# Idle TensorE products where the planned schedule leaves it resting, with newly searched turns

## The chip, the core and the metric

The kernel runs on one core of a Trainium2 chip. The metric is the device time of one execution in microseconds (us); the kernel before took 2129.86 us in the median of five runs (2125.64 to 2135.88). Engines are named as in the profile: PE is TensorE (PEld its weight loads), ACT ScalarE, DVE VectorE, POOL GpSimd, SP the engine that issues most DMAs. All data is float32 but for two bf16 masks.

## The reference, cut to what matters

Sixteen images of 512 tokens by 256 features pass through four layers, each added to its input:

```python
x = x + attention(layernorm(x))   # RMS norm, 16 heads of 16, causal softmax, output projection
x = x + routed(layernorm(x))      # base product + shared low-rank + 2 of 6 low-rank experts
x = x + scan(layernorm(x))        # conv of 4, silu, softplus step, 16-state recurrence, gate, projection
x = x + routed(layernorm(x))
```

The recurrence is `h = decay * h + inp` over the 512 tokens for each of 256 x 16 (feature, state) pairs, summed over states with `ct`.

## The kernel before, in words

All images are recorded as small operations, each with an engine, an estimated cost, the buffers that it reads and writes, and a function that issues its instructions. `Plan.order` then plays these operations through a model of the engines: whenever an engine is free it takes the ready operation with the lowest turn whose buffers are free. A turn is the image's entry in `STARTS` plus the operation's entry in `TURNS`, one list for all sixteen images; both lists, and `OVER` and `CHANGE`, come from a search made elsewhere. The functions are called in the order in which the model started them, and every engine's queue holds its instructions in that order. A few set-up operations (constants, weights, masks: `first`, `for_attention`, `for_routing`, `for_scan`) are issued ahead of the first operation of their stage; the model gives them no time.

PSUM has eight banks: four belong to the one buffer "sc", which holds the scores of four heads, and four to the four buffers "one", which serve everything else: projections, transposes, the sums of the scan and the decays. The tile layer gives each new "one" tile a bank whose old tile has had its last use issued, and adds the semaphore wait for that use. The planner counts free "one" buffers by its own clock.

What an image does, with the lines that matter here:

- Normalisation: VectorE statistics (L490, L491) for attention, ScalarE squares with a running sum (L507) for the other layers, a few GpSimd operations, then the scaled copy on ScalarE (L518: xhA, xhR). PE transposes it (L529), ScalarE copies it out (L532).
- Attention: projections (L480, called from several places), then for each of four groups of four heads the scores in two forms. `four` issues four 32-row products (L603) and four mask products (L605) into "sc". In the first form (sc from kT and qT) VectorE takes the row maxima (L677, negm); in the second (sc from qm and kT) ScalarE takes the exponential (L623, pt). As there is one "sc", PE can start the next scores only when VectorE or ScalarE has read the last. Between them PE does other work: weights by values (L630), transposes (L641, L685, L702), projections of other images.
- Routed layer: low-rank products (L480, low), some twenty tiny VectorE operations (L751 to L785), a transpose (L794), products with base and up (L480), VectorE adds (L558 or L554).
- Scan: conv and gate, then the step (dt) and step times input (sg, GpSimd L857) are stored to DRAM (drows), and fetched again, spread over 16 states (dd, L889 fetches of 512 KB). For each of 16 pieces GpSimd multiplies (L896), ScalarE makes two decays into "one" banks (L901), VectorE scans twice (L904), GpSimd multiplies (L907), and PE sums over states (L914, four products of two pieces), after which the pieces' dd buffers (five) are free for the next fetches.

Up to four images are under way at once, in different layers. The first image starts alone, and the last two end alone.

Of the kernel before, what the change touches and what calls it, by code (L numbers as in the profile page):

```python
# [10 lines left out]
F32 = mybir.dt.float32  # L11
# [6 lines left out]
P = 128  # L18
NEG = -1.0e30


OVER, CHANGE = 1.8, 98.0
STARTS = (
    0, 250, 450, 689, 961, 1201, 1411, 1675, 1928, 2203, 2451, 2680, 2957, 3175, 3503, 3764,
)
TURNS = (
    1486, 1502, 1591, 1805, 1649, 1220, 1616, 1672, 1410, 1613, 1491, 1898, 1583, 1875, 1343, 1506, 1183,
    1541, 1298, 1279, 1375, 1335, 1139, 1347, 1441, 1286, 1157, 1394, 1206, 1565, 1353, 1537, 1379, 1591,
    1379, 1594, 1372, 1651, 1522, 1660, 1365, 1611, 1517, 1583, 1349, 1403, 1398, 1378, 1448, 1325, 1481,
    1454, 1333, 1736, 1548, 1735, 1337, 1438, 1477, 1301, 1523, 1408, 1545, 1447, 1179, 1692, 1501, 1819,  # L30
    1508, 1490, 1586, 1319, 1422, 1542, 1547, 1376, 1572, 1477, 1589, 1287, 1623, 1386, 1700, 1560, 1706,
    1428, 1741, 1547, 1867, 1565, 1751, 1595, 1618, 1381, 1444, 1396, 1117, 1466, 1413, 1505, 1210, 1206,
    1711, 1675, 1808, 1463, 1423, 1594, 1561, 1499, 1404, 1606, 1475, 1396, 1802, 1678, 1811, 1675, 1644,
    1851, 1522, 1400, 793, 1319, 860, 713, 1017, 1032, 632, 724, 538, 935, 830, 973, 723, 927, 594, 796,
    525, 755, 598, 976, 661, 615, 1198, 512, 319, 388, 362, 129, 494, 312, 358, 602, 524, 567, 502, 544,
    859, 531, 746, 681, 561, 1231, 1218, 1194, 538, 729, 790, 1427, 1103, 1044, 704, 1086, 1098, 1018, 922,
    1615, 1327, 2057, 999, 2302, 1044, 1268, 1651, 1845, 1952, 2206, 1645, 1707, 2356, 1737, 1676, 1481,
    1017, 1153, 1270, 1220, 1217, 1026, 1092, 1419, 1470, 1474, 1403, 1419, 1405, 1245, 1447, 1465, 1366,
    1442, 1300, 1587, 1537, 1510, 1358, 1604, 1638, 1487, 1692, 1620, 1552, 1539, 1145, 1320, 1419, 1331,
    1542, 1656, 1715, 1772, 1728, 1673, 1650, 1876, 1677, 1609, 1610, 1726, 1779, 1751, 1778, 1654, 1464,  # L40
    1718, 1712, 1847, 1789, 1885, 1661, 1808, 1754, 1719, 2223, 1692, 1819, 1816, 1845, 1871, 1647, 1629,
    1805, 1577, 1758, 1803, 1893, 1944, 1483, 1819, 2065, 1596, 1989, 1718, 1866, 1889, 1718, 1723, 1901,
    1720, 1771, 1593, 1791, 1958, 1949, 1640, 1816, 1941, 1928, 1937, 1864, 1964, 2028, 1588, 1877, 2140,
    2072, 2032, 1799, 2052, 2224, 2260, 2139, 2353, 2400, 2267, 2365, 2277, 2293, 2410, 1995, 2248, 2295,
    2162, 2168, 1967, 2274, 2187, 2133, 1808, 2013, 2045, 2260, 2318, 2449, 2528, 2408, 2021, 2064, 2097,
    2119, 2019, 1819, 2261, 2249, 1936, 1316, 1929, 1436, 1226, 1471, 1322, 1474, 1422, 922, 1141, 1098,
    836, 1016, 1544, 1086, 1351, 1132, 1480, 1505, 2021, 1951, 1888, 2774, 1677, 1136, 1141, 936, 0, 876,
    507, 1665,
)


# [18 lines left out]
class Plan:  # L70
# [5 lines left out]

    def __init__(self, places):  # L80
        self.places, self.ops, self.seq, self.stage = dict(places), [], 0, 0
# [47 lines left out]
    def order(self):  # L129

        first = {}
        for o in self.ops:
            o.turn = STARTS[o.seq] + (TURNS or [0] * len(self.ops))[o.num - first.setdefault(o.seq, o.num)]
        free, busy, table, link, port, mode = dict(self.places), {}, None, 0.0, False, None
        kept = {}
        ready = {}
        for o in self.ops:
            ready.setdefault(o.eng, [])
            busy.setdefault(o.eng, False)
            if not o.left:  # L140
                bisect.insort(ready[o.eng], (o.turn, o.num, o))
        events, out = [], []
        now, tick = 0.0, 0
        while True:
            for eng, heap in ready.items():
                if busy[eng] or not heap:
                    continue
                until, what = kept.get(eng, (None, None))

                picked, turns = None, heap  # L150
                if eng == "ACT":
                    turns = sorted(heap, key=lambda i: (i[0] + CHANGE * (i[2].table not in (None, table)), i[1]))
                for item in turns:
                    if until is not None and not self.wanted(item[2], what):
                        cost = item[2].cost + 1.3 * (item[2].table not in (None, table))
                        if now + cost > until + OVER:
                            continue
                    need = {}
                    for b in item[2].bufs:
                        if not b.taken:  # L160
                            need[b.res] = need.get(b.res, 0) + 1
                    if not (item[2].port and port) and all(free[k] >= v for k, v in need.items()):
                        picked = item[2]
                        heap.remove(item)
                        break
                if picked is None:
                    continue
                o = picked
                for b in o.bufs:
                    if not b.taken:  # L170
                        b.taken = True
                        free[b.res] -= 1
                cost = o.cost
                if o.table is not None:
                    cost += 1.3 * (o.table != table)
                    table = o.table
                if eng == "PE":
                    cost -= 0.2 * (o.mode is not None and o.mode == mode)
                    mode = o.mode
                if until is not None and self.wanted(o, what):  # L180
                    del kept[eng]
                if isinstance(o.then, Op):
                    kept[o.then.eng] = (now + cost + o.lat, o.then)
                elif o.then is not None:
                    kept[o.then[0]] = (now + cost + o.lat, o.then[1])
                busy[eng] = True
                port = port or o.port
                out.append(o)
                end = now + cost
                done = end + o.lat  # L190
                if o.load:
                    link = max(link, end) + o.load
                    done = link + o.lat
                tick += 2
                heapq.heappush(events, (end, tick, "free", o))
                heapq.heappush(events, (done, tick + 1, "done", o))

            late = [eng for eng, (at, what) in kept.items() if at + 0.3 < now and not busy[eng]]
            for eng in late:
                del kept[eng]  # L200
            if late:
                continue
            if not events:
                if not kept:
                    break
                kept.clear()
                continue
            now = events[0][0]
            while events and events[0][0] <= now:
                _, _, kind, o = heapq.heappop(events)  # L210
                if kind == "free":
                    busy[o.eng] = False
                    if o.port:
                        port = False
                    continue
                for b in o.bufs:
                    b.users -= 1
                    if not b.users:
                        free[b.res] += 1
                for x in o.after:  # L220
                    x.left -= 1
                    if not x.left:
                        bisect.insort(ready[x.eng], (x.turn, x.num, x))
        assert len(out) == len(self.ops), "operations wait for each other's places"
        self.span = now
        return out


@with_exitstack
def tile_block(ctx: ExitStack, tc: tile.TileContext, a: dict, out: bass.AP):  # L230
# [4 lines left out]
    nc = tc.nc  # L235
# [16 lines left out]
    ps = ctx.enter_context(tc.tile_pool(name="ps", bufs=1, space=PSUM))  # L252
# [5 lines left out]
    def tile_of(name, shape, dtype=F32):  # L258
        return const.tile(shape, dtype, name=name)
# [7 lines left out]
    ident, identb = tile_of("ident", [P, P]), tile_of("identb", [P, P], BF)  # L267
# [166 lines left out]
    banks = {"one": (4, [P, 512]), "sc": (1, [P, G, 512])}  # L434
# [3 lines left out]
    plan = Plan(places)  # L438
# [497 lines left out]
    with tc.manual_schedule():  # L936
        done = 0
        for o in plan.order():

            while done < o.stage:  # L940
                setups[done]()
                done += 1
            o.fn()


# [44 lines left out]
```

## Time and profile before

| what | value |
|---|---|
| median of five runs | 2129.86 us (2125.64 to 2135.88) |
| the profiled execution, its time | 2125.51 us |
| its span, first to last instruction | 2123.7 us |
| mean granted TensorE clock | 0.922 of full |
| PE busy | 1810.3 us (85%), 13253 matmul records |
| VectorE, ScalarE, GpSimd busy | 1400.6 (66%), 1292.8 (61%), 1411.0 us (66%) |
| PE's scores L603 waiting for pt L623 | 126.9 us, 105 times |
| PE's scores L603 waiting for negm L677 | 19.9 us, 17 times |
| PE's sums L914 waiting for dd L907 | 43.7 us, 14 times |
| stores of finished images issued (first, thirteenth, last) | 389.9, 1821.7, 2119.9 us |

Times in the profile count from the span's start. A float32 product that isn't a transpose leaves two matmul records, and a record's duration contains the end of its pipeline, so that records overlap. In the views by window, each row gives the busy time of five engines with the number of instructions, the mean granted clock (PEclk, 1.00 is full), the busy share of the DMA engines and GB/s. In a timeline each row gives start, duration, engine, line, operation, tiles, count, and in brackets how long the engine rested before and what ended it. Images are counted from 0.

### The profile page before, as it was taken

The numbers are of one execution on the slowest core, as the hardware profiler recorded it, in microseconds if no ns is written. First come the engines' busy times: TensorE is split into PE (matmuls) and PEld (weight loads), VectorE is DVE, ScalarE is ACT, GpSimd is POOL, SyncE is SP. The second block draws the span as 40 slices with busy tenths as digits, with TensorE's granted clock in tenths as the row PEclk, the third lists the DMA queues.
The fourth block names the chain that finished last, engine by engine and source line by source line (L and its number), as shares of the span: only waits on it lengthen the run. The fifth ranks groups of instructions, "written<-read, shape, count | busy, mean of one in ns | idle before, by whom it ended". The sixth has DMA issues, their size and how long they took to land. (4 is left out here: it accounts for less than half of the span.)

```text
span 2123.7 us, 35012 instructions
## 1 busy us (share of the span) xinstructions
PE 1810.3 (85%) x13253; PEld 983.1 (46%) x13253; DVE 1400.6 (66%) x2351; ACT 1292.8 (61%) x2077; POOL 1411.0 (66%) x846
## 2 busy tenths in 40 slices
PE   4679888999999998999998999999999998986534
PEld 2335354545454454545454454545455454544212
DVE  4224576858767686858767676858767676866462
ACT  2226567575767667676667667575667667664521
POOL 2001585858678585959678695848679585959593
PEclk8769899999999999999999999999999999998756
DMA  3000775939395685849395775939396785859591
GB/s 90 1 1 1 170 171 139 213 93 231 83 225 133 170 197 131 219 101 228 90 213 128 187 182 134 216 96 220 86 213 144 171 198 131 209 129 216 141 218 43
DMA packets 113066, 316.37 MB, mean 149 GB/s; under 512 B 17809, under 2 KB 36610, under 8 KB 112898
## 3 DMA queue, kind: packets, MB, share of 16 engines
q1 hardware_dynamic: 112194, 313.99, 61.4%
q8 instruction: 105, 1.72, 0.4%
q14 instruction: 63, 0.52, 0.1%
q10 hardware_dynamic: 704, 0.14, 0.0%
HBM read 287.87 MB, written 26.21 MB: 148 GB/s over the span
## 5 line engine op out<-in xcount | busy, mean ns | idle before, releaser
L904 DVE TENSOR_TENSOR_SCAN dd<-one,dd 128x512 f32<-128x512 f32 x512 | 611.3, 1213 | 138.0 <-POOL dd L896 50.0
L896 POOL TENSOR_TENSOR dd<-dd,bc 128x1024 f32<-128x1024 f32 x256 | 602.7, 2357 | 128.7 <-DMA dd<-drows 107.3
L907 POOL TENSOR_TENSOR dd<-dd,bc 128x1024 f32<-128x1024 f32 x256 | 602.8, 2357 | 52.5 <-DVE dd L904 48.1
L677 DVE TENSOR_REDUCE negm<-sc 128x4 f32<-128x512 f32 (+3 forms) x256 | 380.0, 1484 | 341.6 <-PE sc L605 340.7
L901 ACT ACTIVATE one<-dd,am 128x512 f32<-128x512 f32 x512 | 343.2, 689 | 180.4 <-DVE dd L904 88.1
L623 ACT ACTIVATE pt<-sc 128x2048 f32<-128x2048 f32 (+3 forms) x256 | 315.8, 1234 | 195.7 <-PE sc L605 195.1
L603 PE MATMUL sc<-qm,kT 32*128 32x512 f32 (+3 forms) x2048 | 227.4, 516 | 131.2 <-ACT pt L623 111.5
L603 PE MATMUL sc<-kT,qT 32*128 32x128 f32 (+3 forms) x2048 | 219.8, 500 | 33.3 <-DVE negm L677 16.8
L605 PEld LDWEIGHTS <-identb 128*128 128x128 bf16 x2048 | 121.6, 101 | 240.5 <-issue 228.2
L914 PE MATMUL one<-dd,ysel 128*32 128x512 f32 x1024 | 172.2, 675 | 43.8 <-POOL dd L907 43.7
L603 PEld LDWEIGHTS sc<-qm,kT 32*128 32x128 f32 x2048 | 86.2, 197 | 232.3 <-ACT pt L623 163.8
L503 POOL TENSOR_SCALAR mv<-sums 128x4 f32<-128x4 f32 x48 | 9.3, 194 | 253.4 <-DVE x L558 253.3
L630 PE MATMUL one<-pt,vv 128*32 128x512 f32 (+3 forms) x2048 | 170.1, 477 | 3.3 <-DVE dd L904 3.1
L507 ACT ACTIVATE xhR<-x,mv 128x256 f32<-128x256 f32 x192 | 95.1, 497 | 89.3 <-POOL mv L503 89.3
L603 PEld LDWEIGHTS sc<-kT,qT 32*128 32x128 f32 x2048 | 84.7, 194 | 125.8 <-DVE negm L677 36.4
L480 PE MATMUL one<-base,xtR 128*128 128x256 f32 x512 | 137.7, 392 | 0.0
L857 POOL TENSOR_TENSOR sg<-dt,xc 128x512 f32<-128x512 f32 x32 | 40.5, 1266 | 145.9 <-ACT dt L852 145.9
L630 PEld LDWEIGHTS one<-pt,vv 128*32 128x32 f32 x2048 | 63.7, 117 | 100.9 <-issue 79.8
L518 ACT ACTIVATE xhR<-x,nm,rs 128x256 f32<-128x256 f32 x192 | 100.8, 591 | 14.5 <-POOL nm L514 14.3
L558 DVE SCALAR_TENSOR_TENSOR x<-one,x 128x256 f32<-128x256 f32 x192 | 72.7, 416 | 55.4 <-PE one L480 55.3
L605 PE MATMUL sc<-mask_k,identb 128*128 128x128 bf16 x1024 | 109.0, 233 | 0.0
L605 PE MATMUL sc<-mask_q,identb 128*128 128x128 bf16 x1024 | 104.9, 227 | 0.0
(138 smaller groups left out, 2620.4 us busy)
## 6 DMA issues: line engine op xcount, KB each, us to landing
dd<-drows SPq DMA_DIRECT2D x512, 512.0 KB
x<-in_x_dram SPq DMA_DIRECT2D x16, 512.0 KB
drows<-dt SPq DMA_DIRECT2D x32, 256.0 KB
drows<-sg SPq DMA_DIRECT2D x32, 256.0 KB
bc<-brows SPq DMA_DIRECT2D x16, 512.0 KB
out_dram<-x SPq DMA_DIRECT2D x16, 512.0 KB
brows<-few SPq DMA_DIRECT2D x16, 64.0 KB
wo<-in_Wo_dram SPq DMA_DIRECT2D x2, 256.0 KB
```

The source lines that it names most:

```text
L480: nc.tensor.matmul(o[:, lo:hi], lhsT=lhsT, rhs=rhs, start=n == 0, stop=n == len(todo) - 1)
L518: op("ACT", act(256) + 0.18, lambda t=t: nc.scalar.activation(xh()[:, t, :], x()[:, t, :], AF.Identity, bias=nm()[:, t, 0:1], scale=rs()[: ...
L603: nc.tensor.matmul(sc()[:, g, 0:n], lhsT=lhsT(g), rhs=rhs(g), start=True, stop=False)
L605: nc.tensor.matmul(sc()[:, g, at : at + P], lhsT=identb, rhs=mask, start=False, stop=True)
L623: o.then = op("ACT", act(G * n), lambda pt=pt, sc=sc, n=n: nc.scalar.activation(pt(), sc()[:, :, 0:n], AF.Exp), r=[sc], w=[pt], table="exp")
L630: nc.tensor.matmul(av()[rows(g), kt * P : T], lhsT=vals()[:, kt, G * j + g, :], rhs=pts[kt]()[:, g, :], start=kt == 0, stop=kt == NT - 1,)
L677: o.then = op("DVE", dve(G * n), lambda t=t, n=n, sc=sc, nm=nm, s=s: nc.vector.tensor_reduce(nm()[:, t, :, 1 - s, 0:1], sc()[:, :, 0:n], A ...
L896: op("POOL", pool(1024), lambda dd=dd: nc.gpsimd.tensor_tensor(dd()[:, :, 1, :], dd()[:, :, 1, :], both(0), ALU.mult), port=True, r=[(bc, ...
L901: op("ACT", act(512) + 0.07, lambda i=i, k=k, dd=dd, dec=dec: nc.scalar.activation(dec(), dd()[:, i, 0, :], AF.Exp, scale=am[:, k + 4 * i ...
L904: op("DVE", 1.22, lambda i=i, dd=dd, dec=dec: nc.vector.tensor_tensor_scan(dd()[:, i, 1, :], dec(), dd()[:, i, 1, :], 0.0, ALU.mult, ALU.a ...
L907: op("POOL", pool(1024), lambda dd=dd: nc.gpsimd.tensor_tensor(dd()[:, :, 1, :], dd()[:, :, 1, :], both(1), ALU.mult), port=True, r=[(bc, ...
L914: nc.tensor.matmul(sums()[rows(g), :], lhsT=ysel[:, m, :], rhs=four[g]()[:, g % 2, 1, :], start=m == 0, stop=m == 3)
```

## The change

Two things change. First, `Plan.order` notes when PE works and how many "one" buffers are free by its own model, and a new method, `resting`, puts idle products into PE's planned rests: one wherever 0.45 us and a margin of 0.1 us are left before the next PE operation, a "one" buffer is free by the model for that long, and PE has worked for less than 72% of the last 3.4 us. When the operations are issued, each PE operation is preceded by its idle products: an identity times two copies of itself (256 columns, float32) into a fresh "one" tile that nothing reads. Second, `STARTS`, `TURNS`, `OVER` (1.8 to 1.9) and `CHANGE` (98 to 115) are new.

```diff
+    SPAN, BUSY, IDLE, EDGE = 3.4, 0.72, 0.45, 0.1
...
+                        if b.res == "one":
+                            room.append((now, free["one"]))
...
+                if eng == "PE":
+                    runs.append((now, end, o))
...
+        self.rests = self.resting(runs, room)
         return out
+
+    def resting(self, runs, room):
+
+        rests, last, at, k = {}, [], 0.0, 0
+        for begin, end, o in runs:
+            while at + self.IDLE + self.EDGE <= begin:
+                while k + 1 < len(room) and room[k + 1][0] <= at:
+                    k += 1
+                i, free = k + 1, room[k][1]
+                while i < len(room) and room[i][0] < at + self.IDLE + self.EDGE:
+                    free = min(free, room[i][1])
+                    i += 1
+                last = [x for x in last if x[1] > at - self.SPAN]
+                worked = sum(b - max(a, at - self.SPAN) for a, b in last)
+                if free > 0 and worked < self.BUSY * self.SPAN:
+                    rests[o.num] = rests.get(o.num, 0) + 1
+                    last.append((at, at + self.IDLE))
+                    at += self.IDLE
+                else:
+                    at += self.EDGE
+            last.append((begin, end))
+            at = max(at, end)
+        return rests
...
+            for _ in range(plan.rests.get(o.num, 0) if done else 0):
+                one = ps.tile([P, 512], F32, tag="one", name="one", bufs=banks["one"][0])
+                nc.tensor.matmul(one[:, 0 : 2 * P], lhsT=ident, rhs=ident.unsqueeze(1).to_broadcast([P, 2, P]), start=True, stop=True)
             o.fn()
```

In the built program 379 idle products stand in 115 runs between 8227 products of before: 18 between the set-up products and the first transposes, and one after those; 42 in the rest of the first image's lone attention; 32 while the pipeline fills; nine per image from image 3 to image 14 (four, one, two and two, always ahead of the same four operations); 15 in the last attention; and 163 in the drain, in runs of up to 21. In the middle each queue's order differs from before in a few exchanges alone: for some pieces of the scan the two halves or two neighbouring pieces change places on all five engines, and a value projection, a pair of transposes and some products move past a neighbour. The number of the other instructions of each kind is the same.

## The prediction

> **What bounds the kernel now.** I read the page's slices first: how busy TensorE (PE) is and which clock it was granted, each slice 53 us.
>
> ```profile
> PE   4679888999999998999998999999999998986534
> ...
> PEclk8769899999999999999999999999999999998756
> ```
>
> PE is at 90% from slice 6 to slice 36, while no other engine passes 80% for long. The clock is low in slices 2 to 4, lowest at the end, and just under full between. So I cut the span at the marks where the work changes (windows view: us, busy time and instructions of PE, PEld, DVE, ACT, POOL, then clock, DMA share, GB/s): opening, first attention alone, filling, twelve like periods between two stores of the result, and the drain.
>
> ```profile
> 0.00:40.10 40.10, 18.28 (x97) 11.06 (x97) 19.44 (x65) 13.08 (x21) 15.54 (x32) 1.00 0.47 119
> 40.10:165.00 124.90, 90.05 (x628) 42.83 (x628) 33.45 (x32) 31.51 (x35) 0.00 (x0) 0.71 0.00 1
> 165.00:389.87 224.87, 197.25 (x1495) 103.92 (x1493) 139.20 (x237) 138.81 (x219) 127.23 (x73) 0.92 0.53 127
> 389.87:1821.67 1431.80, 1315.00 (x9939) 720.09 (x9937) 1041.79 (x1729) 970.58 (x1560) 1055.13 (x624) 0.96 0.68 164
> ...
> 1941.00:2123.70 182.70, 88.53 (x320) 46.44 (x320) 83.80 (x150) 63.45 (x115) 122.93 (x67) 0.67 0.61 143
> ```
>
> What does a lost clock cost? The twelve periods answer it; two of them:
>
> ```profile
> 865.63:982.67 117.04, 106.61 (x831) 58.74 (x829) 86.84 (x145) 80.83 (x130) 87.25 (x53) 1.00 0.69 167
> 982.67:1103.37 120.70, 111.17 (x832) 61.08 (x829) 86.67 (x145) 81.08 (x130) 89.15 (x53) 0.94 0.68 162
> ```
>
> Same work, and only PE's busy time and the clock differ: the period at full clock takes 117.04 us, the mean is 1431.80/12 = 119.32. Where the clock falls, a finer cut shows why. In steps of 3.41 us, the grid on which the clock changes here:
>
> ```profile
> 1064.13:1067.54 3.41, 1.42 (x16) 0.55 (x14) 0.00 (x0) 3.41 (x7) 1.93 (x3) 1.00 1.04 229
> 1067.54:1070.95 3.41, 3.41 (x28) 2.85 (x28) 0.00 (x0) 2.60 (x5) 1.18 (x2) 0.50 1.04 231
> 1070.95:1074.37 3.42, 3.42 (x52) 1.55 (x48) 2.79 (x3) 3.39 (x6) 2.14 (x1) 1.00 1.05 232
> ```
>
> A step with PE busy 1.42 of 3.41 us is followed by one at half clock, a full one by full clock; the period's other poor step, 1077.78 to 1081.19, has 1.75. Over the whole span 47 full-clock steps are followed by half clock, and the busiest of them had 1.95 us; to come back, a half-clock step had to be busy 2.8 us or more. The rests come from the one "sc" place: PE waits for ScalarE to read the scores (in the waits view, sc L603 behind pt L623: 126.9 us in 105 waits).
>
> **The change, part by part.** *Where the products stand.* I set the place of each of the 379 products against the timeline of before. From 40 to 1941 us, 197 of them stand where PE rested: per period four before the scores of 128 columns (rest 1.99 us), one before those of 256 (1.52), two before those of 384 (1.11), two before the next head's first scores (0.87). An idle product is one like value's (L480, 128x256): eight records, four products, took 1.95 us, so (1.95 - 0.38)/7 = 0.22 us a record, two records, 0.45 us; at half clock 0.85 (a 128-column record at half clock: (1.91 - 0.42)/7 = 0.21 in the opening's transposes below; twice as wide and two of them). Four fill 1.8 of 1.99 us: they fit, with the 0.16 us by which a record outlasts its streaming. The two poor steps rise to 1.42 + 1.8 = 3.2 and 1.75 + 0.45 = 2.2 us busy, both over 1.95, so I expect the clock to hold.
>
> *Price of a half-clock microsecond.* The five periods at 0.94 (120.70 to 121.48) average 121.14 us, with 0.06 x 2 x 121.1 = 14.5 us at half clock: (121.14 - 117.04)/14.5 = 0.28 us each. The five at 0.97 average 118.29: 1.25/7.1 = 0.18.
>
> *Opening: +8.* 18 products stand ahead of the first transposes. But PE does not rest there:
>
> ```profile
> 18.80 2.08 PE L480 MATMUL one<-wo,sg 128*128 128x256 f32 x4 [0.64 <-DMA cw<-in_conv_w_dram]
> 20.67 1.91 PE L529 MATMUL one<-ident,xhA 128*128 128x128 f32 x8
> ```
>
> The transposes follow without a rest; ScalarE had their input at 10.7 us, for the set-up products held PE (the plan has no set-up in its time). 0.21 us a 128-column record shows half clock until about 23 us: 2.8 products in 2.4 us, 15.2 at 0.45: 9.2 us, less 0.9 as the transposes then run at full clock. All of image 0 waits for them. Ends: 7.2 (all at full clock, less 0.9) and 15.3 (all at 0.85).
>
> *First attention: -16.* Clock 0.71: 0.29 x 2 x 124.9 = 72 us at half clock. Its rests (36 us in the timeline) get 42 products. 72 x 0.28 = 20, and I count four fifths as recovered. Ends: -6 (0.18 and half of it) and -26 (half of the 52 us that PE is busy in them).
>
> *Filling: -8.* 0.08 x 2 x 224.9 = 36 us at half clock, x 0.23. Ends -3 and -10.
>
> *Twelve periods: -18.* All at 117.04: 12 x 2.28 = -27. Against it stands a new wait. A bank's new tile waits for the last reader of the old one; the second product before the 384-column scores gets the bank of a scan. In the full-clock period:
>
> ```profile
> 961.78 2.34 DVE L904 TENSOR_TENSOR_SCAN dd<-one,dd 128x512 f32<-128x512 f32 x2 [0.84 <-ACT one L901]
> ...
> 962.78 0.93 PE L603 MATMUL sc<-qm,kT 32*128 32x384 f32 x8 [1.11 <-ACT pt L623]
> ```
>
> That scan, first of the two in the new order, ends at 963.0; the product then ends at 963.45, and the scores come 0.67 us late. The product before the 256-column scores waits for a scan ending at 960.33: 960.78 instead of 960.63. Together 0.8 us a period, 12 x 0.8 = +9.6. Behind PE stand all later products, so it counts in full. Ends: 0 and 2.8 us a period (the pair's 2.34 and a product). The exchanges in the orders (which half of a scan pair goes first, on all five queues) leave counts and ScalarE's table loads (76) as they are; I take them at 0, within 1 us a period either way.
>
> *Drain: +9.* 163 products in 19 runs, 73 us in 107 us of rests; but they stand in order behind scans. At the last long run:
>
> ```profile
> 2079.82 1.92 PE L914 MATMUL one<-dd,ysel 128*32 128x512 f32 x4 [7.21 <-POOL dd L907]
> 2084.42 1.93 PE L914 MATMUL one<-dd,ysel 128*32 128x512 f32 x8 [2.68 <-POOL dd L907]
> 2086.99 1.63 PE L914 MATMUL one<-dd,ysel 128*32 128x512 f32 x4 [0.63 <-POOL dd L907]
> ```
>
> 21 stand before the sums that end the seventh group; the fourth waits for the last scan (2084.4), so 18 x 0.45 follow: 2092.5, then two groups at full clock and three products, 3.7 us: 2096.2, where before ended at 2088.6: +7. Likewise 14 before image 15's transposes, the third behind a scan ending 1974.6: 1980, transposes ready at 1976.0: +4 on its whole scan. 14 before image 14's last routing transpose: eight after 2024.5 end at 2028.1, not 2022.3; half of these 6 us reach the sums whose buffers the next fetches need: +3. Later runs stretch the fetches by about 2. Against it, the last 30 us lie at half clock and PE is on the chain there: transposes 1.98 to 1.04, low products 3.78 to 1.96, the last products 6.83 to 5.35, and similar pieces before: -7. Sum +9; ends -7 (no run late) and +20.
>
> **Sum:** 8 - 16 - 8 - 18 + 9 = -25. The profiled execution took 2125.5 us (span 2123.7), 4.4 under the median of 2129.9: 2125.5 - 25 = 2100.5, say 2101, and a median may lie up to 4 us above that.
>
> The Trainium skill ("TensorE: Matmul & The Clock Gate", section "HAM oscillation — how this bites in real kernels") speaks against the change: it gives as the rule that PE falls back when a rest passes about 3.4 us. Here a longest rest of 1.99 us was enough (1.42 busy of 3.41). By that rule the rests of 1 to 2 us would cost no clock and the products bring nothing, as in the last rival below, with its time. The trace decides against it.
>
> **Rivals.** *Cheap products* (0.20): every bank is free in time, as the plan thinks. Opening +8, head -20, filling -10, periods -27, drain -6: -55, 2071. For it: rests and products match. Against it: the scans' ends above.
>
> *The scans' banks become the bound* (0.10), slower. With its clock back PE reaches the rests earlier, while scans are paced by GpSimd and ScalarE; each period both waits then cost a whole pair. At 4 us a period, between one pair with its product (2.8) and two (5.6): 2101 + 12 x 3.2 = 2139. It decides from 0.8 + 25/12 = 2.9 us a period. Against it: in the full-clock period the lateness was 0.8.
>
> *Half the gains* (0.08): 26 of 51 us, since some steps stay poor, with the costs of 8, 10 and 16 less 7: about 2126, no change.
>
> *The products don't hold the clock* (0.06): the gate counts something that they lack. Then only the costs are left: 2125.5 + 8 + 10 + 16 = 2159. Against it: every kind of product lies in the full steps.
>
> **How the numbers follow.** My forecast, 2085 to 2115, has 0.56. Faster by over 0.3% (about what a measurement of this kernel can tell from no change) is under 2123.5: 0.56 + 0.20 = 0.76; within it 0.08; slower 0.10 + 0.06 = 0.16. The range leaves out the two slow cases and a little below 2071: 2066 to 2127.
>
> **What would show it.** Clock 0.98 or more from 165 to 1941 us; a period of 117.8 us; the first transposes at about 29.6 us; first attention 16 us shorter; idle products before the 384-column scores waiting for L904's scan; a drain 9 us longer. It is wrong if the periods stay at 119 with a full clock (coupling), or if half clock follows filled steps.

## The result, and the profile after

The changed kernel takes 2122.5 us in the median of 31 runs (2113.5 to 2128.9), the kernel before 2129.3 us in 55 (2117.0 to 2141.2): ratio 0.9964, with a 95% interval of 0.9952 to 0.9976. It is faster by 0.36%, where 1.35% was forecast. The profiled execution took 2125.38 us (span 2123.6), nearly what that of before took (2125.51, span 2123.7), so the two profiles are compared stage by stage. All lines of before come back 36 higher (L904 is L940, L914 is L950, L603 is L639); the idle product is L981.

The page's slices, TensorE's busy share and granted clock:

```profile
PE   5889999999999999999999999999999899887777
...
PEclk9999999999999999999999999999999999998988
```

The clock is there nearly everywhere (mean 0.977, was 0.922), and PE is busier in the first three slices and in the last four. The same stages as before, cut at about the same marks of the work (windows view: us, then busy time and instructions of PE, PEld, DVE, ACT, POOL, clock, DMA share, GB/s):

```profile
0.00:40.10 40.10, 21.40 (x91) 16.21 (x95) 15.01 (x62) 9.96 (x17) 15.62 (x32) 1.00 0.46 119
40.10:150.00 109.90, 91.47 (x739) 49.04 (x732) 35.97 (x33) 34.45 (x40) 0.00 (x0) 0.97 0.00 1
150.00:371.40 221.40, 203.85 (x1580) 112.03 (x1578) 139.79 (x239) 139.88 (x219) 126.87 (x73) 1.00 0.54 129
371.40:1789.20 1417.80, 1325.56 (x10160) 738.91 (x10152) 1041.91 (x1730) 972.20 (x1561) 1055.43 (x625) 0.99 0.69 166
1908.50:2123.60 215.10, 160.17 (x668) 107.88 (x667) 85.62 (x158) 66.26 (x124) 126.09 (x69) 0.87 0.52 125
```

The first image is stored at 371.4 us instead of 389.9 (-18.5; forecast 8 - 16 - 8 = -16). The twelve periods take 1417.8 us instead of 1431.8 (-14; forecast -18). The drain, from the thirteenth store to the end, takes 334.4 us instead of 302.0: +32.4, where +9 was forecast with an upper end of +20. So nearly the whole gain came, and the drain took nearly all of it back. The last row is the drain's second part. It is not cut quite like the row of before (182.7 us, clock 0.67): that one begins 6 us behind the last attention's end, this one 2 us ahead of it. Counted from that end, the rest of the kernel took 188.4 us at clock 0.68 before and takes 212.9 us at 0.86 now. More clock, and more time. The other 8 us of the drain's 32 lie ahead of that end (113.7 us from the thirteenth store before, 121.4 now).

A full-clock period, one of the four that still lose time, and the poor step in that one:

```profile
843.70:961.00 117.30, 109.71 (x854) 61.21 (x846) 86.77 (x146) 81.01 (x131) 88.10 (x53) 1.00 0.68 168
...
723.40:843.70 120.30, 111.74 (x854) 62.09 (x846) 86.75 (x145) 80.96 (x131) 87.13 (x52) 0.97 0.68 162
```

```profile
748.49:751.90 3.41, 1.55 (x24) 0.77 (x16) 2.52 (x16) 3.16 (x7) 3.33 (x5) 1.00 0.80 222
751.90:755.31 3.41, 1.76 (x3) 1.00 (x4) 2.02 (x4) 2.03 (x4) 3.41 (x2) 0.51 1.04 240
```

The timeline of PE there shows why the step was not filled (start, duration, ..., in brackets the rest before and what ended it):

```profile
750.32 0.50 PE L639 MATMUL sc<-qm,kT 32*128 32x128 f32 x8 [1.11 <-ACT pt L659]
750.75 0.40 PE L641 MATMUL sc<-mask_k,identb 128*128 128x128 bf16 x4
753.49 2.08 PE L981 MATMUL one<-ident 128*128 128x256 f32 x3 [2.34 <-DVE dd L940]
```

The product that should fill the rest waits 2.34 us for a scan, and the clock falls at 751.90. Four periods (120.4, 120.8, 119.5, 120.5 us) keep one half-clock stretch of 6.8 us each; the eight others average 117.1 us.

The opening, where 18 products now stand ahead of the first transposes, which started at 20.67 us before:

```profile
20.81 9.96 PE L981 MATMUL one<-ident 128*128 128x256 f32 x36
30.61 1.04 PE L565 MATMUL one<-ident,xhA 128*128 128x128 f32 x8
```

**The drain.** Where the forecast looked at the seventh group of the last image's scan, the timeline of all engines shows now:

```profile
2076.76 2.34 DVE L940 TENSOR_TENSOR_SCAN dd<-one,dd 128x512 f32<-128x512 f32 x2 [6.21 <-POOL dd L932]
...
2078.04 11.41 PE L981 MATMUL one<-ident 128*128 128x256 f32 x40 [6.15 <-DVE dd L940]
2079.24 2.34 POOL L943 TENSOR_TENSOR dd<-dd,bc 128x1024 f32<-128x1024 f32 x1 [0.21 <-DVE dd L940]
...
2089.37 1.06 PE L950 MATMUL one<-dd,ysel 128*32 128x512 f32 x8
```

The run of idle products waits 6.15 us for a scan's bank; the scan's result, multiplied by GpSimd, is ready for the sums (L950) at 2079.24 + 2.34 = 2081.6; but the sums stand behind 20 products and start at 2089.4, 7.8 us late. The chain of waits shows that this happens group after group, and what the groups do to each other (start, duration, what):

```profile
2023.60 7.60 PE one L981 x22
2031.20 1.05 PE one L950 x8
...
2034.13 10.08 DMA dd<-drows
...
2045.04 1.06 DVE dd L940
...
2046.23 0.68 PE one L981 x2
2046.91 0.04 issue
2046.95 5.56 PE one L981 x24
2052.52 1.06 PE one L950 x8
...
2054.87 7.79 DMA dd<-drows
```

Products hold the sums, the sums hold the dd buffers, so the next fetch starts late; the fetched piece is scanned late; and the next run of products waits for that scan. In this loop each delay is handed on instead of being covered. The waits view of the same stretch (1910 to 2123.6 us; total, times, longest) adds that the products also hold banks which ScalarE's decays (L937) want:

```profile
ACT one L937 <- PE one L981: 35.8, 5, 9.2
...
DVE gate L956 <- PE one L950: 29.0, 4, 14.0
PE one L981 <- DVE dd L940: 27.2, 9, 6.1
```

### The profile page after: what moved, and what is told of

It is laid out like the page before. It is cut to its first block, busy times and chain, and to the rows that moved or that the text cites. A ratio compares the mean times of both kernels' runs of the same rounds, so it can differ in the third digit from the quotient of the medians.

```text
span 2123.6 us, 36559 instructions
## 1 busy us (share of the span) xinstructions
PE 1909.2 (90%) x14011; PEld 1085.1 (51%) x14011; DVE 1399.9 (66%) x2351; ACT 1295.7 (61%) x2077; POOL 1411.7 (66%) x846
## 5 line engine op out<-in xcount | busy, mean ns | idle before, releaser
L940 DVE TENSOR_TENSOR_SCAN dd<-one,dd 128x512 f32<-128x512 f32 x512 | 607.5, 1212 | 162.1 <-ACT one L937 95.4
L937 ACT ACTIVATE one<-dd,am 128x512 f32<-128x512 f32 x512 | 344.5, 689 | 242.8 <-DVE dd L940 117.3
L981 PE MATMUL one<-ident 128*128 128x256 f32 x758 | 228.3, 435 | 70.2 <-DVE dd L940 55.8
L639 PE MATMUL sc<-qm,kT 32*128 32x512 f32 (+3 forms) x2048 | 210.3, 480 | 69.2 <-ACT pt L659 52.2
L641 PEld LDWEIGHTS <-identb 128*128 128x128 bf16 x2048 | 116.3, 98 | 225.9 <-issue 211.0
L639 PE MATMUL sc<-kT,qT 32*128 32x128 f32 (+3 forms) x2048 | 212.6, 485 | 14.9 <-DVE negm L713 10.7
L981 PEld LDWEIGHTS one<-ident 128*128 128x128 f32 x758 | 147.0, 212 | 124.0 <-DVE dd L940 58.5
L639 PEld LDWEIGHTS sc<-qm,kT 32*128 32x128 f32 x2048 | 80.0, 182 | 171.7 <-ACT pt L659 112.2
L666 PE MATMUL one<-pt,vv 128*32 128x512 f32 (+3 forms) x2048 | 158.8, 452 | 2.1 <-DVE dd L940 2.1
L950 PE MATMUL one<-dd,ysel 128*32 128x512 f32 x1024 | 138.7, 604 | 2.9 <-POOL dd L943 2.9
L639 PEld LDWEIGHTS sc<-kT,qT 32*128 32x128 f32 x2048 | 81.2, 185 | 114.8 <-DVE negm L713 46.2
```

Source lines behind the costliest of these rows:

```text
L639: nc.tensor.matmul(sc()[:, g, 0:n], lhsT=lhsT(g), rhs=rhs(g), start=True, stop=False)
L641: nc.tensor.matmul(sc()[:, g, at : at + P], lhsT=identb, rhs=mask, start=False, stop=True)
L666: nc.tensor.matmul(av()[rows(g), kt * P : T], lhsT=vals()[:, kt, G * j + g, :], rhs=pts[kt]()[:, g, :], start=kt == 0, stop=kt == NT - 1,)
L937: op("ACT", act(512) + 0.07, lambda i=i, k=k, dd=dd, dec=dec: nc.scalar.activation(dec(), dd()[:, i, 0, :], AF.Exp, scale=am[:, k + 4 * i ...
L940: op("DVE", 1.22, lambda i=i, dd=dd, dec=dec: nc.vector.tensor_tensor_scan(dd()[:, i, 1, :], dec(), dd()[:, i, 1, :], 0.0, ALU.mult, ALU.a ...
L950: nc.tensor.matmul(sums()[rows(g), :], lhsT=ysel[:, m, :], rhs=four[g]()[:, g % 2, 1, :], start=m == 0, stop=m == 3)
```

## The experiments

Theory: the drain's 32 us come from the 163 products after the last attention, by the loop above; head and periods keep their gain without them. Rivals: the new order lengthens the drain (A), or the new order made the gain (B); something else in the drain is late, and the late products pay for themselves by the clock (C); it is PE's own time for the products, not the bank's wait (D). The two kernels and the twelve variants stand in one table: idle products; median; ratio to the kernel before on the same chip; and from each one's profile the first store, the mean of the twelve periods, and the drain (thirteenth store to the end), in us.

| kernel | products | median | ratio (95%) | first store | period | drain |
|---|---|---|---|---|---|---|
| before | 0 | 2129.3 | 1 | 389.9 | 119.32 | 302.0 |
| changed | 379 | 2122.5 | 0.9964 (0.9952 to 0.9976) | 371.4 | 118.15 | 334.4 |
| e1 order alone | 0 | 2128.8 | 1.0006 (0.9981 to 1.0030) | 392.8 | 119.25 | 308.8 |
| e2 none late | 216 | 2097.2 | 0.9853 (0.9813 to 0.9894) | 370.6 | 118.42 | 306.2 |
| e3 late in sc | 379 | 2102.7 | 0.9883 (0.9845 to 0.9922) | 368.9 | 118.75 | 311.9 |
| e4 turns of before | 343 | 2122.3 | 0.9969 (0.9946 to 0.9992) | 364.7 | 117.86 | 338.4 |
| e5 late in sc, in turn | 379 | 2090.7 | 0.9818 (0.9793 to 0.9844) | 370.8 | 118.81 | 296.2 |
| e6 no opening, none late | 198 | 2092.6 | 0.9831 (0.9807 to 0.9854) | 359.6 | 118.34 | 305.4 |
| e7 as e6, more in periods | 289 | 2100.9 | 0.9860 (0.9835 to 0.9884) | 363.0 | 118.24 | 309.7 |
| e8 no opening, late in turn | 361 | 2081.0 | 0.9766 (0.9740 to 0.9791) | 359.2 | 118.38 | 299.1 |
| e9 as e8, turns of before | 325 | 2078.6 | 0.9759 (0.9728 to 0.9789) | 361.4 | 117.90 | 303.3 |
| e10 late runs of three | 264 | 2098.3 | 0.9848 (0.9823 to 0.9874) | 369.1 | 117.98 | 311.6 |
| e11 as e8, five a period | 313 | 2084.7 | 0.9796 (0.9758 to 0.9833) | 362.5 | 118.61 | 295.4 |
| e12 as e8, none in periods | 252 | 2099.5 | 0.9858 (0.9825 to 0.9891) | 363.3 | 119.28 | 297.7 |

**e1, the order alone.**

```diff
-        self.rests = self.resting(runs, room)
+        self.rests = {}
```

> The changed kernel with its new STARTS, TURNS, OVER and CHANGE, but without a single idle product. Theory (the new order is worth nothing by itself; all that moved comes from the products, and the 32.4 us that the drain lost too): it behaves as the kernel before, drain (thirteenth store to the end) 302 us within 5, period 119.3 within 0.5, clock about 0.92, 2125 to 2133 us. Rival A (the new order lengthens the drain, the products only restore the clock): the drain stays at 325 us or more and the time is 2145 to 2165. Rival B (the new order brought the gain of the periods): period 118.2 with the clock at 0.96, time 2110 to 2118.

No difference to before (ratio 1.0006); periods 119.25 at clock 0.96. The profile's drain, 308.8 us, is 6.8 over before, two more than the theory allowed. So the order brings nothing, and rivals A and B fall for the time as a whole; a few us of the drain may be the order's.

**e2, no product after the last attention.**

```diff
-            for _ in range(plan.rests.get(o.num, 0) if done else 0):
+            for _ in range(plan.rests.get(o.num, 0) if done and spent < 216 else 0):
+                spent += 1
```

> The changed kernel with its first 216 idle products, up to the end of the last attention, and without the 163 that follow. Theory (the late products give the gain back: they stand in PE's queue behind scans of the pieces under way, hold the four banks, and make sums, fetches and decays late): thirteenth store issued at 1789 within 4, drain back at about 302, so 2089 to 2099 us, 23 to 33 under the changed kernel, ratio to before 0.981 to 0.986. Rival A (order): drain stays at 325 or more, 2115 to 2130. Rival C (the late products paid for themselves through the clock and something else in the drain is late): 2115 to 2135, as the clock at the end falls back to 0.67.

2097.2 us, as the theory had it: the drain is back to 306.2 us, at half clock as before. The late products cost 28 us of drain net, clock gained included (25 us by the medians). The 4 us by which this drain is still longer than that of before come ahead of the last attention's end, 120.0 us behind the thirteenth store: that part is some 6 to 8 us longer than before with the new order alone (119.6 in e1), with the products alone (121.4 in e4) and with both, so the late products have no share in it. The row of the drain's second part (cut just ahead of the last attention's end), beside which stands 215.1 us at 0.87:

```profile
1911.00:2097.90 186.90, 93.99 (x334) 48.42 (x332) 84.21 (x154) 66.21 (x123) 124.22 (x68) 0.68 0.61 144
```

**e3 and e5, the late products in the banks of the scores.** After the last attention nobody uses the four banks of "sc"; e3 gives each late product a new "sc" tile and writes its first bank, e5 takes the four banks in turn.

```diff
+                if spent > 216:
+                    one = ps.tile([P, G, 512], F32, tag="sc", name="sc", bufs=banks["sc"][0])[:, 0, :]
```

```diff
+                if spent > 216:
+                    sc = sc if j else ps.tile([P, G, 512], F32, tag="sc", name="sc", bufs=banks["sc"][0])
+                    one = sc[:, j % G, :]
```

> All 379 idle products at their places, but the 163 late ones write the four banks of the scores, which nobody uses once the last attention has ended, in place of a bank of one. So they wait for no reader and hold no bank that decays or sums want; PE's time for them stays. Theory: no L940 scan and no other reader stands ahead of a late product, and the clock of the drain is kept; drain 290 to 300 us, time 2079 to 2092. Rival D (it is PE's own time for the products, 0.57 to 0.70 us each in long runs where the plan has 0.45, that makes the sums late): drain 318 to 334, time 2107 to 2123. Rival A (order): the same as D.

> All 379 idle products, the 163 late ones into the four banks of the scores as in the run of that name, but in turn, one bank after the other. There each late product took 0.757 us from start to start, since it waited for its predecessor in the same bank (48.2 us in 105 waits in the drain), 9.8 us for a run of 13 where the planned rest is 8 to 12 us. Theory (what was left of the drain's loss there was PE's own time for the products, blown up by that wait): with 0.45 us each a run of 13 takes 5.9 us and fits, the clock stays at 0.98, drain 297 to 304 us, 2088 to 2096 us. Rival D' (even so the runs make the sums late, or the sums are late for another reason): 2100 to 2106 as before.

e3 lay between the two: 2102.7 us, drain 311.9. Its timeline shows 13 products in 9.78 us, 0.75 us each, and the sums directly behind them:

```profile
2008.08 9.78 PE L985 MATMUL sc<-ident 128*128 128x256 f32 x26
2017.79 1.06 PE L950 MATMUL one<-dd,ysel 128*32 128x512 f32 x8
```

Each product waits for the one before it in the same bank. In turn, in e5, 13 take 5.88 us (0.45 each, the plan's figure), and the sums wait for GpSimd again, as they did before the change:

```profile
2036.10 5.88 PE L987 MATMUL sc<-ident 128*128 128x256 f32 x26
2041.90 1.05 PE L950 MATMUL one<-dd,ysel 128*32 128x512 f32 x4
2044.28 1.12 PE L950 MATMUL one<-dd,ysel 128*32 128x512 f32 x4 [1.32 <-POOL dd L943]
```

With that the drain is 296.2 us, the shortest but one of all, and its second part has the clock:

```profile
1915.80:2092.70 176.90, 144.66 (x660) 98.57 (x658) 84.55 (x154) 66.17 (x123) 124.55 (x68) 0.98 0.65 152
```

Same products, same places, other banks: 334.4 - 296.2 = 38 us are the waits for banks, and against e2 the clock that the products bring is worth 10 us. These are sizes from single profiles; the medians give 32 and 6.5 us. The thirteenth store of e5's profile comes 7 us later than the changed kernel's, though nothing differs ahead of it, so single profiles differ by that much. D holds only where products wait for each other (16 us of drain, e3 against e5), and C falls: without the late products it had 2115 us or more, and e2 took 2097.2.

**e4, the turns of before with the new products.** The two lists and two constants of before stand in the changed kernel.

> The turns, starts, OVER and CHANGE of before with the new resting: 343 idle products where that order leaves PE resting by the plan. Theory (products alone make both sides): first store 10 to 22 us earlier than before, period 117.5 to 118.7, drain 18 to 35 us longer than 302, time 2112 to 2128. Rival B (the new order is needed for the gain): periods stay at 119 or more, time over 2130.

2122.3 us: the change's result without its new turns. First store 25 us earlier than before, drain 36 us longer, both a little more than expected.

**e6 and e7, the opening and the periods.** e6 is e2 without the first 18 products; e7 is e6 with BUSY 0.88, and leaves out its first 22 products and the late ones. The two diffs show e6's condition and e7's constant.

```diff
+                if spent <= 18 or spent > 216:
+                    continue
```

```diff
-    SPAN, BUSY, IDLE, EDGE = 3.4, 0.72, 0.45, 0.1
+    SPAN, BUSY, IDLE, EDGE = 3.4, 0.88, 0.45, 0.1
```

> No late products, and without the first 18 too, which stand ahead of the first image's transposes: 198 idle products. Theory (the opening term of the forecast: these products make the first transposes 8 us late and all follows): 2086 to 2092 us, 8 under the 2097.2 of the kernel with 216, first transposes at about 22 us. Rival (the opening products pay for themselves by the clock of the first transposes and projections, or the start is hidden behind something else): 2094 to 2099.

> As the kernel without opening and late products, but BUSY is 0.88 in place of 0.72, so that up to the last attention 289 idle products stand in place of 198: seven more in each period from other rests too. Theory (the four of twelve periods that still take about 120.5 us have a step that is too little filled): all twelve periods at 117 to 117.5, 10 to 16 us less than the kernel without opening products, 2074 to 2081 us. Rival (more products wait for more scans, as the rival of the forecast had it): periods of 118 or more at full clock, 2089 to 2105 us.

e6: the first transposes start at 20.92 us instead of 30.61 and the first image is stored 11 us earlier than in e2. The median is only 4.6 lower and just outside what was expected, with intervals that overlap; e8 against e5, the same edit, gives 0.5% or 11 us. e7 refutes its theory, and its time is the rival's: eleven of its twelve periods are at 1.00, and yet they average 117.9 us (the changed kernel's eight: 117.1); the twelfth, at 0.97, takes 122.5 us. The median is 8 us worse than e6's. The row holds all twelve, 118.24 us each; its clock is rounded:

```profile
363.00:1781.90 1418.90, 1347.14 (x10272) 755.10 (x10264) 1041.77 (x1729) 971.07 (x1561) 1054.51 (x625) 1.00 0.69 166
```

**e8 and e9, both cures.** No opening products, and late ones in turn in the scores' banks; e9 with the turns of before.

```diff
+            late = late or o.seq == B - 1 and o.num % per >= 119
+            sc, n = None, plan.rests.get(o.num, 0) if done and o.num not in (11, 13) else 0
...
+                if late:
+                    sc = sc if j else ps.tile([P, G, 512], F32, tag="sc", name="sc", bufs=banks["sc"][0])
+                    one = sc[:, j % G, :]
```

> The changed kernel without the 18 products ahead of the first transposes, and with the late products in turn in the four banks of the scores: 361 idle products. Theory (the two costs are separate and add up): first store at about 360 as without the opening products, period 118.3 to 118.8, drain 296, so about 2081 us (2075 to 2087). Rival (one of the two gains depends on the other): 2088 to 2094, as each alone.

> The same two edits with the turns, starts, OVER and CHANGE of before: 325 idle products. Theory (the order brings nothing; the products' places and banks decide): first store at 354 to 358, periods near 117.9 as with these turns before, drain 292 to 300, so 2068 to 2080 us, no worse than with the new turns. Rival B' (the new turns serve the products): slower than with the new turns by 5 us or more.

2081.0 and 2078.6 us: the two cures add up, and the order does not matter (e9's first store and drain came out some 3 us over what was expected, its time within). Both beat the kernel before by 2.3 to 2.4%, and the changed one by 2%.

**e10, late runs of three at most,** still in the banks of "one".

```diff
+            for _ in range(min(n, 3) if late else n):
```

> The changed kernel with its opening products and at most three idle products in a run after the last attention, 48 late ones in place of 163, still in the banks of one. Theory (it is the products behind a waiting one that make the sums late: a run of 3 has 1 us of them where a run of 13 has 5 and more, and it takes at most three of the four banks): drain 303 to 314, 2095 to 2106 us. Rival E (one wait on a scan is enough to set off the loop through sums, fetches and the next scan, however short the run): drain 320 or more, over 2110 us.

2098.3 us, drain 311.6: short runs do no great harm, as the theory had it, and one wait on a scan is not enough to set off the whole loop. The run does not show which it is that costs in the long runs, the products queued behind the waiting one or the banks that they take, for both are fewer here. The short runs bring nothing either: e2 without them has 306.2.

**e11 and e12, what the products in the periods are worth.** e8 with fewer products for images 3 to 14: e11 without the pairs ahead of the 384-column scores and the next head's first, e12 without all nine.

```diff
+            n = 0 if 2 < o.seq < B - 1 and o.num % per in (74, 107) else n
```

```diff
+            n = 0 if 2 < o.seq < B - 1 and not late else n
```

> The kernel with both edits (no opening products, late ones in turn in the scores' banks, 2081.0 us) without the two pairs a period that most often wait for a scan: those ahead of the 384-column scores and of the next head's first scores. Five products a period are left, 313 in all. Theory (the pairs cost nothing when they wait, as full-clock periods took 117.1 us with them; what is lost in four of twelve periods is that the pair comes 2.3 us late and its step stays too poor): without them that step is poor more often, periods 119 to 120, 2088 to 2100 us. Rival (their waits for scans hold PE up, as the forecast had it, 0.8 us a period or more): periods 117.5 or less, 2066 to 2076 us.

> The kernel with both edits, without any product of images 3 to 14 in the twelve periods; head, filling, last image and drain keep theirs, 252 in all. Theory (the nine a period bring the clock and 0.9 to 1.2 us a period, and this adds to the rest): periods 119.0 to 119.6, 2090 to 2096 us. Rival (in the periods the products bring nothing, the gain there was chance): periods 118.4, 2079 to 2084 us.

e12: periods of 119.28, as before the change, so nine products a period are worth 0.9 us a period in the profiles; the medians differ by more (18 us). The twelve periods of e12, then of e8:

```profile
363.30:1794.70 1431.40, 1306.25 (x9944) 719.56 (x9936) 1042.15 (x1730) 971.81 (x1561) 1057.11 (x625) 0.96 0.69 164
```

```profile
359.20:1779.70 1420.50, 1328.46 (x10160) 739.85 (x10152) 1041.59 (x1730) 972.10 (x1561) 1055.52 (x625) 0.99 0.69 166
```

e11: 118.61 and 2084.7 us, between its theory and its rival. The pairs bring something, but within the intervals. In its profile the periods hold 78 us at half clock, in e8's 31: that the pairs hold the clock is seen, that their waits cost nothing is not shown.

## Why the prediction was wrong, point by point

- **What bounds the kernel, price of a half-clock us, where the products stand: right.** Filled steps hold the clock (0.99 in the periods, 0.97 in the first attention). The 1.95 us of before is no sharp bound, though. In the changed kernel a full-clock step with PE busy 2.12 us is followed by half clock:

```profile
48.76:52.17 3.41, 2.12 (x27) 1.26 (x26) 1.38 (x2) 0.00 (x0) 0.00 (x0) 1.00 0.00 0
52.17:55.58 3.41, 3.41 (x15) 1.52 (x15) 1.23 (x1) 0.00 (x0) 0.00 (x0) 0.51 0.00 0
```

The price, 0.18 to 0.28, may have been somewhat high: e8's periods hold 78 us less at half clock than e12's and take 10.9 us less, 0.14 us each, with the products' waits in it; the medians (18 us) would make it 0.24.

- ***Opening: +8.* Right in kind, somewhat small.** First transposes at 30.6 us (forecast 29.6), 9.7 us later than without the products (e6). In the first store they cost 11 us (e2 against e6), inside the stated ends.
- ***First attention -16, filling -8.* Somewhat small.** Without the opening products the first image is stored 30 us earlier than before (359.6 in e6 against 389.9), where 24 were forecast. That the first store of the changed kernel, -18.5, lies so near the forecast -16 is in part luck: the two misses, 6 us and 3 us, have opposite signs.
- ***Twelve periods: -18.* Right in size (-14), wrong in its cost term.** The waits for scans came, and were longer than forecast: PE's products waited 23.8 us in 18 waits, 2.0 us a period. But the eight full-clock periods average 117.1 us, what the one period of before at full clock took (117.04), so there these waits seem to lie in rests that PE has anyway and to cost next to nothing instead of 0.8 us a period; no run takes them away with the clock kept. Their price is another: a product that waits fills nothing. In four periods the step before it stayed poor, and these took 3.2 us more. So the sum is near although its cost term is not the one that was forecast. That more products cost at full clock, as the rival of the scans' banks had it, is what e7 suggests: 0.8 us a period with sixteen (117.9 against 117.1).
- ***Drain: +9.* This step failed; measured +32.4.** The single piece that was worked out with care came out close: sums 7.8 us late at the last long run (forecast 7; its own numbers, 2096.2 less 2088.6, give 7.6). What failed is how the pieces were put together. The forecast counted the two early runs as 4 and 3 us, and "Later runs stretch the fetches by about 2". Measured from the thirteenth store, the last image's first sums end at 220.0 us in the changed kernel and at 207.0 in e2, without late products (before: 203.7): 13 us where 7 were counted. From there to its last sums the scan takes 83.7 us, in e2 64.2 and in e5 62.9 (before: 63.2): 20 us where 9 were counted (7 for the last run and the 2). Together that is 33 us where 16 were counted. The first and last sums in the changed kernel, then in e2:

```profile
2008.15 1.06 PE L950 MATMUL one<-dd,ysel 128*32 128x512 f32 x8
...
2091.86 1.07 PE L950 MATMUL one<-dd,ysel 128*32 128x512 f32 x8
```

```profile
1996.78 1.94 PE L950 MATMUL one<-dd,ysel 128*32 128x512 f32 x8
...
2060.99 1.88 PE L950 MATMUL one<-dd,ysel 128*32 128x512 f32 x4 [0.64 <-POOL dd L943]
```

The sums free the dd buffers that the next fetches need, and the next scan is what the next run waits for, so each run's lateness becomes the next one's wait. The clock gain that was counted for the end came (behind the last sums 30.7 us are left instead of 35.1). Ahead of them part of it was lost, for a waiting product does not keep the clock: 0.87 where the same products in free banks have 0.98 (e5). The bound of +20 had no term for this loop.

- **The new turns, set at 0: right** for the whole (e1, e9), with up to 7 us of the drain in one profile.

Among the rivals, *The scans' banks become the bound* named the right resource, and put it in the periods instead of the drain. *Half the gains* named the nearest time, about 2126 us, but for a reason that did not hold: nearly the whole gain came, and the drain took it back.

Two readings of the slices (counted from 1) were loose: PE's slices 5 to 7 are at 8, not 9, and the low clock of the head is in slices 2, 3 and 5, not 4. No term rests on them.

The Trainium skill ("TensorE: Matmul & The Clock Gate", section "A second HAM failure mode: psum-queue depth-cycling") describes a kernel whose clock swings because PE rests briefly but often between groups of products, while it cycles through banks. The step at 748.49 us agrees: 1.55 of 3.41 us busy, a rest of 1.11 us for ScalarE and then one for a bank, and half clock after it.

What stays open: why e7 and e12 have medians 8 and 18 us over their neighbours when their profiled executions, which are the fastest of those two kernels, stand only 6.5 and 13.6 us over those of e6 and e8; and how the 38 us of bank waits divide between products ahead of sums and products in banks that decays want (35.8 us of ScalarE's waits), which no run separates.

## What to carry to other kernels

Filler work in an engine's queue was cheap here only where it could start the moment the engine rested: give it a buffer that no other engine's late work reads, and rotate it so that it does not wait for itself. Put in order, ask of each filler what it waits for and what is queued behind it; where that feeds back into the thing it waits for, add up the loop and not the single delay. Where a chain has no slack, at the start and in the drain, weigh each filler against what stands behind it, since there it adds its own time.

## What the runs showed of the hardware that was not expected

- A float32 product of 256 columns took 0.45 us in a run that takes four banks in turn, and 0.75 us in a run that always writes the same bank (each new tile there waits for the product before).
- TensorE's clock does not by itself decide the time: e7's eleven periods at 1.00 average 117.9 us, the changed kernel's eight at 1.00 average 117.1; and the changed kernel's drain was longer at 0.87 than before at 0.67.
